# Rows of ones and zeros, a moved split and a new filler in a two-layer graph kernel

## The chip, the cores and the metric

The kernel runs on one core of a Trainium2 chip. The metric is the device time of one execution in microseconds (us), as a median of runs. The core's engines are named as in its profile: PE (matrix multiplication; PEld is its loading of weights), DVE (vector), ACT (scalar), POOL (which issues the gathers) and SP (which issues most other transfers).

## The reference

A graph of 12500 nodes with 256 features and 200000 edges passes through two layers that average over incoming edges, a last linear layer, a residual and a normalization of each row:

```python
def _sage_conv(x, src, dst, W_l, b_l, W_r):
    msgs = x[src]
    agg = jax.ops.segment_sum(msgs, dst, num_segments=N_NODES)
    deg = jax.ops.segment_sum(jnp.ones((src.shape[0],), x.dtype), dst, num_segments=N_NODES)
    mean = agg / jnp.maximum(deg, 1.0)[:, None]
    return mean @ W_l + b_l + x @ W_r

h = jax.nn.relu(_sage_conv(x, src, dst, W1_l, b1, W1_r))
h = jax.nn.relu(_sage_conv(h, src, dst, W2_l, b2, W2_r))
return _layernorm(x + (h @ W3 + b3))
```

All is float32. The edges come sorted by `dst`, which is drawn as 12500 times the square of a uniform number, so nodes with low numbers have many incoming edges; `src` is uniform.

## The kernel before

Nodes lie in 98 blocks of 128, edges in tiles of 128. There are two ways to sum the messages.

**Dense, for the nodes with many edges** (the first 1280 in layer 1, the first 1792 in layer 2), in groups of 256 nodes. `count` makes a matrix of counts, how often each source node occurs for each target node of the group, tile by tile (748 tiles over the groups): DVE makes 0/1 rows `pick` (L661: 128 partitions by w rows of 98, w being 5, 7 or 9; it says which target and which block of sources an edge has), `low` (L665: which of the 128 sources in the block; four tiles at once) and `aft` (L671: edges whose target is the one that the next tile begins with; four tiles at once). PE multiplies them into `count_ps` (L691, L706, L710), and ACT copies that into `counts` (L712; for the first 128 tiles DVE adds it, L697). `product` multiplies the counts with the table of features (L638), which lies in DRAM as three bf16 parts that add up to the float32 value (`x3_d` for x, `h3_d` for the hidden layer); the parts are made by `exact` (ACT copies at L617 and L619, DVE subtractions at L618 and L620). Each product begins with a multiplication by zero (L631), loads `rows` for two blocks at a time (L635), and has three buffers for them. `degrees` (L728) adds the counts up.

**Gathers, for all other edges.** A round gathers four tiles of 128 messages with four indirect transfers on POOL (L243) into one of four `got` buffers. PE adds each up with a 0/1 matrix (L254, `part_ps`), ACT copies the result (`some`, L259), PE sums it to nodes (L265), and DVE adds it to a ring of eight blocks (`sums`, L277). In layer 1 a further column of ones gives the degrees (L270, and L273 on DVE to the row `degs`). The first rounds of layer 1 run during the setup.

**Blocks.** When a block's sums are complete, `first_block` (layer 1, three pieces) or `last_block` (layer 2, five) computes the layer for it: transposes on PE (L839) that ACT copies (`own_t`, L842), in layer 1 the degree row turned into a column by PE (L886) with its maximum and reciprocal on DVE (L889, L890), the multiplications (L863, L865), bias and relu (L868 to L871), the stores of h and of its three parts (L896, L899), in layer 2 the last linear layer (L921) and the normalization.

**Order.** The order of PE and POOL is written out by hand; that of DVE, ACT and SP is left to a scheduler. `layer` (L562) goes through the rounds. Each round has three turns; a turn takes one piece of a block that is due, and then filler from a list of stages, as much as a written cost allots to the round. In layer 1 stage 0 is the count of group 0 together with the splitting of x (`split_rows`, 98 blocks, L622); stages 1 to 5 are the dense product and degrees of one group beside the count of the next, and the storing of counts for layer 2. Layer 2 has seven stages, one dense product each, beside the count of the last group or the loading of stored counts. The filler's costs are constants (L737: 0.7 for a block of the dense product, 1.6 for 14 matmuls of the degrees, 0.8 for a split), joined by `mixed` (L746) and spread evenly over a layer's rounds:

```python
due = dense_cost * min(1.0, (i + 1 - i0) / (n - i0 - 8))
```

Of the kernel before, what the change touches and what calls it, by code (L numbers as in the profile page):

```python
# [1 line left out]

# [5 lines left out]
F32 = mybir.dt.float32  # L8
# [13 lines left out]
P = 128  # L22
# [25 lines left out]
def by_runs(  # L48
# [79 lines left out]
    h3_d = dram.tile([P, NB, 3, D], BF16, name="h3_d")  # L128
    count_d = dram.tile([HG1 - 1, P, NB, DN], BF16, name="count_d")
# [7 lines left out]
    low_t = consts.tile([P, HC * P], BF16, name="low_t")  # L137
# [3 lines left out]
    after_t = [consts.tile([P, n], F16, name=f"after_t{g}") for g, n in enumerate(tiles_of)]  # L141
# [4 lines left out]
    steps = consts.tile([P, WIDEST * NB], F16, name="steps")  # L146
# [69 lines left out]
    class Gathers:  # L216
# [45 lines left out]
        def summed(self, gr, some, two, done):  # L262
# [6 lines left out]
            if self.width > D:  # L269
                nc.tensor.matmul(sum_ps[0:1, NC], lhsT=some[:, D:D + 1], rhs=two,  # L270
                                 start=True, stop=True)
                deg = degs[:, bass.ds(n0, P)]
                nc.vector.tensor_add(deg, deg, sum_ps[0:1, NC])  # L273
# [5 lines left out]
    with tc.tile_pool(name="setup", bufs=1) as su, \  # L279
# [154 lines left out]
        nc.vector.tensor_copy(steps, steps_f)  # L434
# [127 lines left out]
    def layer(gathers, block, n_pieces, dense, dense_cost):  # L562
# [26 lines left out]
        filler = dense(waiting)  # L589
# [8 lines left out]
        begun = gathers.hot // P  # L598
        for i in range(i0, n + 1):
            before = gathers.step()  # L600
            due = dense_cost * min(1.0, (i + 1 - i0) / (n - i0 - 8))
            for part in range(3):
# [6 lines left out]
                fill(spent + (due - spent) / (3 - part))  # L609
# [11 lines left out]

    def split_rows(b):  # L622
        t = load_rows(x, N, b, "split_sb")
        s = work.tile([P, 3, D], BF16, name="parts")
        exact(t, s, t)
        nc.sync.dma_start(x3_d[:, b], s)

    def product(g, table3, c_sb):

        ps = dense_pool.tile([P, NC, DN], F32, name="dense_ps")  # L630
        nc.tensor.matmul(ps, lhsT=zeros_b, rhs=c_sb[:, :NC, :DN], start=True, stop=False)  # L631
        for b in range(NB):
            if b % 2 == 0:
                rows = work.tile([P, 2, 3, D], BF16, name="rows", bufs=3)
                nc.sync.dma_start(rows, table3[:, b:b + 2])  # L635
# [5 lines left out]
            yield COST_DENSE  # L641
# [4 lines left out]
    def count(g, to):  # L646
# [6 lines left out]
        fours = {}  # L653

        def pick(t):
# [5 lines left out]
            nc.vector.tensor_scalar(r[:, :w * NB], steps[:, :w * NB],  # L661
                                    key_t[g][:, t - lo_g:t - lo_g + 1], None, op0=OP.is_equal)
            if t % G == 0:
                low = work.tile([P, G, P], BF16, name="low")
                nc.vector.tensor_tensor(  # L665
                    low, low_t[:, t:t + G].unsqueeze(2).to_broadcast([P, G, P]),
                    lane_b.unsqueeze(1).to_broadcast([P, G, P]), op=OP.is_equal)
                aft = None
                if t + G >= FIRST:
                    aft = work.tile([P, G, NB], BF16, name="aft")  # L670
                    nc.vector.tensor_tensor(  # L671
                        aft, after_t[g][:, t - lo_g:t - lo_g + G].unsqueeze(2).to_broadcast([P, G, NB]),
                        steps[:, :NB].unsqueeze(1).to_broadcast([P, G, NB]), op=OP.is_equal)
                fours[t // G] = low, aft
            low, aft = fours[t // G]
            return r, low[:, t % G], None if aft is None else aft[:, t % G]

        before = None
        for t in range(lo_g, highs[g]):
# [6 lines left out]
            if t < FIRST:  # L686
# [13 lines left out]
                yield count_cost(t)  # L700
            else:
                n0 = off_act.at(t)
                for a, b in halves:
# [10 lines left out]
                    yield count_cost(t) / len(halves)  # L714
# [7 lines left out]
    def degrees(g, c_sb):  # L722
# [3 lines left out]
        for j in range(DN // P):  # L726
            for b in range(NB):
                nc.tensor.matmul(ps[:, 0, j:j + 1], lhsT=c_sb[:, b, j * P:(j + 1) * P], rhs=ones_b,  # L728
                                 start=b == 0, stop=b == NB - 1)
                if b % 14 == 13:  # L730
                    yield COST_DEGREES
# [5 lines left out]
    COST_DENSE, COST_DEGREES, COST_SPLIT = 0.7, 1.6, 0.8  # L737
# [8 lines left out]
    def mixed(*parts):  # L746

        costs = [c for _, c in parts]
        scale = (max(costs) + 0.3 * (sum(costs) - max(costs))) / sum(costs)
# [568 lines left out]
```

## Time and profile before

| | |
|---|---|
| median of 10 runs | 3413.87 us (3406.39 to 3431.78) |
| the profiled execution, its own time | 3425.84 us |
| its span, from the first to the last instruction | 3424.0 us |
| mean granted PE clock | 0.860 |
| busy: PE, DVE, ACT, POOL | 2600.4, 1463.4, 1238.1, 2045.3 us |
| gathers (L243), layer 1 and layer 2 | 1076 of 1023 ns, 988 of 954 ns |
| moved from and to memory | 582.80 MB read, 89.87 MB written |

In the groups of instructions a line has the source line, the engine, the operation, output and inputs with their sizes, the count, then the busy time in us with the mean of one in ns, and after the second bar the idle time of the engine just ahead of these instructions, with what ended most of it. A line of waits has the waiting instruction, what it waited for, the total in us, the number of waits and the longest. The row PEclk has the granted clock in 40 slices of the span, in tenths of full speed.

### The profile page before, as it was taken

The numbers are of one execution on the slowest core, as the hardware profiler recorded it, in microseconds if no ns is written. First come the engines' busy times: TensorE is split into PE (matmuls) and PEld (weight loads), VectorE is DVE, ScalarE is ACT, GpSimd is POOL, SyncE is SP. The second block draws the span as 40 slices with busy tenths as digits, with TensorE's granted clock in tenths as the row PEclk, the third lists the DMA queues.
The fourth block names the chain that finished last, engine by engine and source line by source line (L and its number), as shares of the span: only waits on it lengthen the run. The fifth ranks groups of instructions, "written<-read, shape, count | busy, mean of one in ns | idle before, by whom it ended". The sixth has DMA issues, their size and how long they took to land.

```text
span 3424.0 us, 54100 instructions
## 1 busy us (share of the span) xinstructions
PE 2600.4 (76%) x18630; PEld 1709.4 (50%) x18630; DVE 1463.4 (43%) x4350; ACT 1238.1 (36%) x2702; POOL 2045.3 (60%) x2074
## 2 busy tenths in 40 slices
PE   3565547878878889889975677778778788878885
PEld 1132225546545656556653444445555565656664
DVE  5667565444444445555442123333223233333333
ACT  0323555555555555565552014333111121211212
POOL 5675655666665665665663666666666666655551
PEclk8576668888979989989987988888889999999998
DMA  4454568648648658757743665666778787766762
GB/s 114 134 148 149 167 202 271 200 144 276 201 149 270 214 156 273 214 149 224 221 136 113 193 206 175 187 191 211 244 237 253 243 252 244 242 202 207 217 203 68
DMA packets 408133, 676.44 MB, mean 198 GB/s; under 512 B 59659, under 2 KB 266537, under 8 KB 407849
## 3 DMA queue, kind: packets, MB, share of 16 engines
q1 hardware_dynamic: 303415, 400.51, 37.9%
q0 software_dynamic: 99072, 270.66, 26.3%
q8 instruction: 149, 2.44, 0.3%
q10 hardware_dynamic: 5362, 1.72, 0.3%
q14 instruction: 135, 1.11, 0.1%
HBM read 582.80 MB, written 89.87 MB: 196 GB/s over the span
## 4 chain that ended last, share of the span: by engine, by line
PE 64%; issue 10%; another core or an unknown queue 8%; DVE 7%; ACT 5%; DMA 4%; ACTq 1%; SPq 0%; DVEq 0%
PE dense_ps L638 21%; PE part_ps L254 9%; PE block_ps L863 7%; PE count_ps L706 6%; PE block_ps L865 5%; PE sum_ps L265 4%; PE block_ps L839 3%; PE block_ps L921 3%; ACT counts L712 2%; PE sum_ps L270 2%; DMA rows<-x_d 1%; PE count_ps L710 1%; DMA rows<-h_d 1%; PE block_ps L886 1%
## 5 line engine op out<-in xcount | busy, mean ns | idle before, releaser
L243 POOL DMA_INDIRECT got<-in_x_dram,src_t x1076 | 1100.5, 1023 | 702.0 <-issue 261.9
L243 POOL DMA_INDIRECT got<-h_d,src_t x988 | 942.7, 954 | 616.1 <-issue 287.1
L638 PE MATMUL dense_ps<-counts,rows 128*128 128x256 bf16 x7056 | 1022.2, 285 | 71.7 <-issue 39.7
L712 ACT CAST counts<-count_ps 128x392 f32 (+2 forms) x1052 | 716.7, 682 | 522.2 <-PE count_ps L710 117.8
L638 PEld LDWEIGHTS <-rows 128*128 128x128 bf16 x7056 | 686.1, 102 | 362.0 <-issue 176.3
L706 PE MATMUL count_ps<-pick,low 128*128 128x392 bf16 (+2 forms) x1052 | 364.4, 370 | 142.0 <-ACT counts L712 63.7
L254 PE MATMUL part_ps<-got,one 128*32 128x257 f32 (+1 forms) x4128 | 399.6, 446 | 93.1 <-ACT some L259 30.4
L661 DVE TENSOR_SCALAR pick<-steps,key_t 128x686 bf16<-128x686 f16 (+2 forms) x748 | 298.6, 410 | 215.1 <-PE count_ps L706 55.9
L201 DVE TENSOR_TENSOR one<-lo_t,lane_b 128x128 f32<-128x128 bf16 x516 | 147.9, 287 | 564.8 <-PE part_ps L254 106.2
L259 ACT COPY some<-part_ps 128x257 f32<-128x257 f32 (+1 forms) x361 | 136.1, 377 | 647.0 <-remote 169.1
L277 DVE TENSOR_TENSOR sums<-sums,sum_ps 128x256 f32 x361 | 148.3, 411 | 297.3 <-remote 118.1
L265 PE MATMUL sum_ps<-two,some 128*128 128x128 f32 x1444 | 245.9, 295 | 4.9 <-issue 4.7
L265 PEld LDWEIGHTS sum_ps<-two,some 128*128 128x128 f32 x1444 | 211.7, 207 | 35.5 <-issue 20.3
L254 PEld LDWEIGHTS part_ps<-got,one 128*32 128x32 f32 x4128 | 92.5, 115 | 254.3 <-issue 170.8
L706 PEld LDWEIGHTS <-low 128*128 128x128 bf16 x1052 | 105.3, 103 | 186.4 <-issue 87.5
L842 ACT COPY own_t<-block_ps 128x256 f32<-128x256 f32 (+1 forms) x294 | 109.8, 377 | 216.8 <-PE block_ps L839 64.6
L868 DVE TENSOR_TENSOR own<-block_ps,biases 128x256 f32<-128x256 f32 x196 | 82.6, 422 | 206.6 <-PE block_ps L865 86.8
L863 PE MATMUL block_ps<-w2l_sb,sums 128*128 128x256 f32 x336 | 115.7, 477 | 46.0 <-DVE sums L277 37.4
L863 PE MATMUL block_ps<-w1l_sb,sums 128*128 128x256 f32 x352 | 125.2, 485 | 30.7 <-DVE sums L277 15.0
L921 PE MATMUL block_ps<-w_sb,own_t 128*128 128x256 f32 x392 | 117.1, 425 | 41.4 <-ACT own_t L842 24.8
L665 DVE TENSOR_TENSOR low<-low_t,lane_b 128x512 bf16<-128x512 bf16 x187 | 128.0, 685 | 42.8 <-PE count_ps L710 13.7
L871 ACT ACTIVATE h<-own 128x256 f32<-128x256 f32 x196 | 81.4, 415 | 174.9 <-DVE own L869 94.9
(180 smaller groups left out, 2614.5 us busy)
## 6 DMA issues: line engine op xcount, KB each, us to landing
rows<-h_d SPq DMA_DIRECT2D x343, 384.0 KB
rows<-x_d SPq DMA_DIRECT2D x245, 384.0 KB
count_d<-counts SPq DMA_DIRECT2D x28, 896.0 KB
counts<-count_d SPq DMA_DIRECT2D x28, 896.0 KB
x_sb<-in_x_dram SPq DMA_DIRECT2D x194, 128.0 KB
x_d<-parts SPq DMA_DIRECT2D x98, 192.0 KB
h_d<-parts SPq DMA_DIRECT2D x98, 192.0 KB
got<-in_x_dram,src_t POOLq DMA_INDIRECT x1076
```

The costliest lines, as they stand in the source:

```text
L201: nc.vector.tensor_tensor(one, lo[:, a:a + n * (G - 1) + 1:n].unsqueeze(2).to_broadcast([P, G, W]), lane_b[:, :W].unsqueeze(1).to_broadcas ...
L243: nc.gpsimd.indirect_dma_start(out=g[:, j, :D], out_offset=None, in_=self.table, in_offset=bass.IndirectOffsetOnAxis(ap=src_t[:, e:e + 1], ...
L254: nc.tensor.matmul(part_ps[j * W:(j + 1) * W, :width], lhsT=one[:, j], rhs=g[:, j, :width], start=r == 0, stop=r == n - 1)
L265: nc.tensor.matmul(sum_ps[:, c], lhsT=some[:, c * P:(c + 1) * P], rhs=two, start=True, stop=True)
L277: nc.vector.tensor_add(own, own, sum_ps[:, :NC])
L638: nc.tensor.matmul(ps[:, c], lhsT=rows[:, b % 2, k, c * P:(c + 1) * P], rhs=c_sb[:, b, :DN], start=False, stop=b == NB - 1 and k == 2 and ...
L661: nc.vector.tensor_scalar(r[:, :w * NB], steps[:, :w * NB], key_t[g][:, t - lo_g:t - lo_g + 1], None, op0=OP.is_equal)
L706: nc.tensor.matmul(ps[:, :(b - a) * NB], lhsT=s, rhs=r[:, a * NB:b * NB], start=True, stop=alone)
L712: nc.scalar.copy(to[:, :, bass.ds(n0 + a, b - a)], ps[:, :(b - a) * NB].rearrange("p (d s) -> p s d", s=NB))
L863: nc.tensor.matmul(ps[:, 0], lhsT=agg[:, c], rhs=wl[:, c], start=c == 0, stop=c == NC - 1)
L865: nc.tensor.matmul(ps[:, 1], lhsT=own_t[:, c], rhs=wr[:, c], start=c == 0, stop=c == NC - 1)
L921: nc.tensor.matmul(y[:, 0], lhsT=h2_t[:, c], rhs=w3_sb[:, c], start=c == 0, stop=c == NC - 1)
```

## The change

Four things are changed, in this order in the diff.

First, the degree sums in layer 1 read the upper halves of their float32 operands as bf16, so that the fp32 matmul becomes a bf16 one. The degree row of a block no longer becomes a column by a matmul with one: it is stored to DRAM (`deg_d`) and loaded as a column two turns later, and the maximum and the reciprocal follow another two turns later.

Second, `pick`, `low` and `aft` are each made for one tile by an operation with one source tensor and a scalar per partition. The sources lie in rows with a gap of two elements after each (`steps` in rows of 98, `lanes_5` in five rows of 26, `steps_7` in seven rows of 14); the output is one run. The scalars of low and aft become float32.

Third, x is split during the first dense product: `product` takes its rows from a function that gives them for two blocks, ahead by one pair; for the first group the function makes the split, hands the tile to PE and stores it to `x3_d`.

Fourth, the filler's share for each round comes from a model of the load of PE, DVE and ACT for each stage and each round (`paced`), and the parts of a stage advance in equal shares (`in_turn`). Further, the `own` tile has two buffers, which `z` shares, and `h_sb` shares the tag of `split_sb`.

```diff
-    low_t = consts.tile([P, HC * P], BF16, name="low_t")
+    low_t = consts.tile([P, HC * P], F32, name="low_t")
-    steps = consts.tile([P, WIDEST * NB], F16, name="steps")
+    steps = consts.tile([P, WIDEST, NB + 2], F16, name="steps")
+    LW = 130
+    lanes_5 = consts.tile([P, 5, LW // 5 + 2], F16, name="lanes_5")
+    steps_7 = consts.tile([P, 7, NB // 7 + 2], F16, name="steps_7")
...
             if self.width > D:
-                nc.tensor.matmul(sum_ps[0:1, NC], lhsT=some[:, D:D + 1], rhs=two,
+                nc.tensor.matmul(sum_ps[0:1, NC], lhsT=some[:, D:D + 1].bitcast(BF16)[:, 1:2],
+                                 rhs=two.bitcast(BF16).rearrange("p (n h) -> p n h", h=2)[:, :, 1],
                                  start=True, stop=True)
...
-        filler = dense(waiting)
+        filler = staged(stages, waiting)
...
+        upto = [left_after(g) if r == groups[g][1] - 1 else 0 for g, r in gathers.rounds]
+        upto = [max(begun, *upto[:i + 1], 0) for i in range(n)]
+        base = [[a + x / groups[g][1] + (upto[i] - upto[max(i - 12, 0)]) / 12 * y
+                 for a, x, y in zip((0.68, 0.29, 0.0), (0.7, 0.95, 0.38), of_block)]
+                for i, (g, r) in enumerate(gathers.rounds)]
+        due = paced(stages, base[i0:n - 8])
         for i in range(i0, n + 1):
             before = gathers.step()
-            due = dense_cost * min(1.0, (i + 1 - i0) / (n - i0 - 8))
+            upto = due[min(i - i0, len(due) - 1)]
...
+    def loaded_rows(table3, b):
+        rows = work.tile([P, 2, 3, D], BF16, name="rows", bufs=3)
+        nc.sync.dma_start(rows, table3[:, b:b + 2])
+        return rows
+
     def split_rows(b):
-        t = load_rows(x, N, b, "split_sb")
-        s = work.tile([P, 3, D], BF16, name="parts")
-        exact(t, s, t)
-        nc.sync.dma_start(x3_d[:, b], s)
-
-    def product(g, table3, c_sb):
+        rows = work.tile([P, 2, 3, D], BF16, name="rows", bufs=3)
+        for k in range(2):
+            t = load_rows(x, N, b + k, "split_sb")
+            exact(t, rows[:, k], t)
+        nc.sync.dma_start(x3_d[:, b:b + 2], rows)
+        return rows
+
+    def product(g, rows_of, c_sb, whole):
...
+        following = rows_of(0)
         for b in range(NB):
             if b % 2 == 0:
-                rows = work.tile([P, 2, 3, D], BF16, name="rows", bufs=3)
-                nc.sync.dma_start(rows, table3[:, b:b + 2])
+                rows, following = following, rows_of(b + 2) if b + 2 < NB else None
...
-            nc.vector.tensor_scalar(r[:, :w * NB], steps[:, :w * NB],
+            nc.vector.tensor_scalar(r[:, :w * NB].rearrange("p (d s) -> p d s", s=NB), steps[:, :w, :NB],
                                     key_t[g][:, t - lo_g:t - lo_g + 1], None, op0=OP.is_equal)
-            if t % G == 0:
-                low = work.tile([P, G, P], BF16, name="low")
-                nc.vector.tensor_tensor(
-                    low, low_t[:, t:t + G].unsqueeze(2).to_broadcast([P, G, P]),
-                    lane_b.unsqueeze(1).to_broadcast([P, G, P]), op=OP.is_equal)
...
+            low = work.tile([P, LW], BF16, name="low", bufs=6)
+            nc.vector.tensor_scalar(low.rearrange("p (a b) -> p a b", a=5), lanes_5[:, :, :LW // 5],
+                                    low_t[:, t:t + 1], None, op0=OP.is_equal)
+            aft = None
+            if t + 1 >= FIRST:
+                aft = work.tile([P, NB], BF16, name="aft", bufs=6)
+                nc.vector.tensor_scalar(aft.rearrange("p (a b) -> p a b", a=7), steps_7[:, :, :NB // 7],
+                                        after_t[g][:, t - lo_g:t - lo_g + 1], None, op0=OP.is_equal)
+            return r, low[:, :P], aft
...
-    COST_DENSE, COST_DEGREES, COST_SPLIT = 0.7, 1.6, 0.8
+    COST_DENSE, COST_DEGREES = 0.7, 0.4
...
+    OF_DENSE = (NB * 0.7, 0.0, 0.6)
+    OF_DEGREES = (5.5, 0.0, 0.0)
+    OF_SPLITS = (0.0, NB * 0.82, NB * 0.75)
+    MOST_LOAD = (0.95, 0.88, 0.9)
...
+    def paced(stages, rounds):
+        loads = [[sum(x) for x in zip(*l)] for _, l in stages([])]
+        def by_rounds(length):
+            at, s = [], 0.0
+            for base in rounds:
+                left = 1.0
+                while s < len(loads) and left > 1e-9:
+                    of = loads[int(s)]
+                    speed = min((length * m - b) / f for m, b, f in zip(MOST_LOAD, base, of) if f)
+                    if speed <= 0:
+                        break
+                    step = min(speed * left, int(s) + 1 - s)
+                    left -= step / speed
+                    s = int(s) + 1 if step == int(s) + 1 - s else s + step
+                at.append(s)
+            return at
...
     def first_block(b, agg=None):
         x_sb = load_rows(x, N, b, "x_sb")
         of_ring = agg is None
-        yield True
-        ps = turned()
         if of_ring:
             overlap(b, True)
             agg, deg_row = ring(b)
-            nc.tensor.matmul(ps[:, NC, 0:1], lhsT=deg_row, rhs=ones[0:1, 0:1], start=True, stop=True)
-        x_t, deg = transposed(x_sb, ps, "own_t", int(of_ring))
+            nc.sync.dma_start(deg_d[b:b + 1], deg_row)
+        yield True
+        if of_ring:
+            deg = work.tile([P, 1], F32, name="deg")
+            with nc.allow_non_contiguous_dma(reason="a row becomes a column"):
+                nc.sync.dma_start(deg, deg_d[b, :, None])
+        x_t = transposed(x_sb, turned(), "own_t")
+        yield True
         if of_ring:
             nc.vector.tensor_scalar(deg, deg, 1.0, None, op0=OP.max)
             nc.vector.reciprocal(rdeg[:, b:b + 1], deg)
-        yield True
         h, own = sage(x_t, b, agg, w1l_sb, w1r_sb, biases[:, 0], "h")
...
-    layer(gathers_1, first_block, 3, staged(stages_1), cost_of(stages_1))
-    layer(Gathers(h_d, True), last_block, 5, staged(stages_2), cost_of(stages_2))
+    layer(gathers_1, first_block, 3, stages_1, (2.35, 2.0, 2.0))
+    layer(Gathers(h_d, True), last_block, 5, stages_2, (3.6, 2.6, 1.75))
```

## The prediction

> **What bounds the kernel now.** I read the page first: the shares, the slices and the chain that ended last. Then the stretches between the zero matmuls that open each dense product (L631), for busy time by stage; then the groups by shape, for prices; then the waits and the timeline around single steps.
>
> ```profile
> span 3424.0 us, 54100 instructions
> PE 2600.4 (76%) x18630; PEld 1709.4 (50%) x18630; DVE 1463.4 (43%) x4350; ACT 1238.1 (36%) x2702; POOL 2045.3 (60%) x2074
> PEclk8576668888979989989987988888889999999998
> PE 64%; issue 10%; another core or an unknown queue 8%; DVE 7%; ACT 5%; DMA 4%; ACTq 1%; SPq 0%; DVEq 0%
> ```
>
> PE carries 64% of the chain, but is not full: it is busy 76% of the span, and the clock row is low where it is least busy.
>
> ```profile
> core 0: us, PE busy (x) PEld busy (x) DVE busy (x) ACT busy (x) POOL busy (x), PEclk, DMA share, GB/s
> 90.00:300.00 210.00, 131.11 (x592) 54.63 (x596) 141.43 (x414) 59.29 (x106) 142.24 (x131) 0.65 0.49 146
> 300.00:491.00 191.00, 109.28 (x583) 51.72 (x576) 129.75 (x354) 116.80 (x244) 112.37 (x107) 0.70 0.53 161
> 491.00:716.00 225.00, 167.11 (x1228) 108.95 (x1228) 111.81 (x328) 114.29 (x230) 127.67 (x125) 0.86 0.77 236
> 716.00:778.00 62.00, 43.59 (x403) 26.20 (x403) 26.51 (x80) 32.98 (x70) 39.46 (x40) 0.72 0.38 113
> 1278.00:1475.00 197.00, 179.62 (x1366) 123.42 (x1366) 100.18 (x297) 111.16 (x238) 119.00 (x121) 0.97 0.79 243
> 1475.00:1539.00 64.00, 50.13 (x442) 30.89 (x442) 31.71 (x99) 37.50 (x77) 40.86 (x42) 0.81 0.42 121
> ```
>
> The first two rows are stage 0 of layer 1 (splits of x and counts of group 0), the next two stage 1 (dense part, then degrees), the last two stage 4. Four gathers on POOL make a round, so the rows give the time of a round: a dense stretch 197/(121/4) = 6.5 us, a degree stretch 64/(42/4) = 6.1. By PE's program order stage 0 holds 57 rounds (401 us, 7.0 each), stage 1 40 (287, 7.2), stages 2 to 5 163 (1075 with a tail of 53 us without gathers: 6.27 each), layer 2 247 (1571, tail 85). So rounds have nearly one length however much filler they hold, and stages 0 and 1 have the longest ones: there PE is waiting (busy .60 in stage 0, where DVE has .68).
>
> ```profile
> POOL got L243 <- PE part_ps L254: 252.3, 87, 19.0
> SPq L626 <- DVE parts L620: 233.0, 35, 92.5
> DVE own_t L889 <- ACT own_t L842: 44.8, 37, 9.9
> ```
>
> POOL waits for PE to free the `got` buffers (252 us in 87 waits): PE sets the pace, not the gathers. Two gathers start 1.25 us apart where nothing holds them (0.95 busy, 0.30 issue): 5 us a round.
>
> **The counts' rows.**
>
> ```profile
> L661 DVE TENSOR_SCALAR pick<-steps,key_t 128x490 bf16<-128x490 f16 x252 | 85.3, 359 | 37.3 <-PE count_ps L710 9.2 <-PE count_ps L706 8.6 <-issue 7.2
> L661 DVE TENSOR_SCALAR pick<-steps,key_t 128x882 bf16<-128x882 f16 x212 | 98.6, 467 | 73.8 <-PE count_ps L706 23.7 <-PE part_ps L254 14.2 <-PE block_ps L839 8.9
> L665 DVE TENSOR_TENSOR low<-low_t,lane_b 128x512 bf16<-128x512 bf16 x187 | 128.0, 685 | 42.8 <-PE count_ps L710 13.7 <-PE count_ps L706 8.1 <-PE part_ps L254 7.6
> L671 DVE TENSOR_TENSOR aft<-after_t,steps 128x392 bf16<-128x392 f16 x156 | 87.1, 558 | 0.0
> L270 PE MATMUL sum_ps<-two,some 128*1 128x128 f32 x372 | 77.0, 292 | 0.0
> L886 PE MATMUL block_ps<-ones,degs 1*128 1x1 f32 x176 | 39.3, 290 | 93.3 <-DVE own L869 49.9 <-issue 11.5 <-DVE degs L273 11.4
> L362 DVE CAST dst_f<-dst_i 128x1664 f32<-128x1664 int32 x1 | 1.0, 1019 | 0.0
> ```
>
> A pick costs 0.28 ns an element now ((467-359)/392). The source gets rows with gaps, an odd number of them, against one run in the output. No row shows this form. Bounds: as now (no cost), or the 1.06 ns of low and aft ((685-558)/120). Between lie the casts: 1664 elements 1019 ns, 1280 elements 827 ns, so 0.50 ns an element and 187 fixed. I take the casts, as the nearest one-source operation that isn't at the quickest rate: picks of 490, 686 and 882 then cost 432, 530 and 628 ns, 392 us for 252 + 284 + 212, against 299: +94. Low becomes 748 operations on 130 elements (252 ns by the casts: 188 us against 128, +60), aft 621 on 98 (236 ns: 147 against 87, +60). DVE +214 in all. By the lower bound (two 128x128 tensor-scalars of the setup took 201 ns) it is about +60, by the upper (1.06 ns and 187 fixed for all) 675-299, 243-128 and 181-87, about +586.
>
> [...]
>
> Off the path: DVE is busy .50 in stage 4; with the 120-tile share of +214 (34 us) it is .63. In stage 0 it is 271 of 401 us; the splits leave (98 x 0.85 = 83), nine rounds leave (about 11), 236 tiles' share comes (+68): 245 us, in 307 (below) .80, still covered. [...] Gathers took 1023 ns in layer 1 and 954 in layer 2; were the picks the cause, 0.07 x 1076 = 75 us of POOL's time come back, which isn't late; I take none.
>
> **The degrees.** L270's 372 fp32 passes become 186 bf16 matmuls: 77 us of PE to 186 x 0.22 = 41 (0.22 us is the mean of the nearest bf16 matmul, aft's 128x98 of L710), 36 saved, between nothing, if light rounds keep their length anyway, and 77. Of the 186 groups 133 lie in stages 2 to 5 (83 groups of two rounds come first, then 103 of one): 26 us there. L886 leaves PE with its 93 us of waits on DVE: 33 of them in stage 0, 32 in stage 1, 20 in stages 2 to 5 where gathers run. In place of it each of 88 blocks issues on SP a 512-byte store behind DVE's add and a 4-byte-packet load. What is queued behind that store on SP: rows loads, h_d and h3_d stores, x_sb loads; PE's dense product waits for rows, but three buffers hold two pairs ahead. A small load takes 2.5 us from issue to use (the split's, shown below: 546.23 to 548.72), the pair about 5; the block asks for the result four turns later (four thirds of a round, 8.4 us). I take 0. Upper bound: SP's longest hold at a rows load is 10.9 us; 10.9 + 5 - 8.4 = 7.5, for a block in four 165 us. Lower bound: 0, as PE's side is counted already.
>
> **The splits move.** Stage 0 loses 98 splits with their 98 loads and 98 stores; SP's 233 us of waits on their last subtraction shrink with them, and PE's one wait of 10 us behind ACT's part of a split in stage 0. Stage 1 gets them, per pair of blocks: two loads, eight operations on ACT and DVE, one store in place of two, and no reading back (49 loads of 384 KB fall away; PE waited 9 us for them). The timeline of stage 1 shows one block's chain from load issue to last subtraction:
>
> ```profile
> 546.23 0.45 SPq L833 DMA_DIRECT2D split_sb<-in_x_dram  x1
> 548.72 0.40 ACT L617 CAST parts<-split_sb 128x256 bf16<-128x256 f32 x1 [0.74 <-DMA split_sb<-in_x_dram]
> 550.27 0.43 DVE L620 TENSOR_TENSOR parts<-split_sb,parts 128x256 bf16<-128x256 f32 x1 [0.35 <-ACT parts L619]
> ```
>
> That is 550.70 - 546.23 = 4.5 us. With two buffers the second block's chain overlaps the first's by half: 4.5 + 2.3 = 6.8 a pair. One pair is emitted ahead. Price: 49 x 6.8 = 331 us for stage 1.
>
> **The filler.** A new pacing moves the stages: by PE's program order after, stage 0 has 48 rounds, stage 1 48, stages 2 to 5 164, layer 2 247. Degree stretches, which were allotted 10 rounds for 196 matmuls of 25 ns, get fewer.
>
> **The sum** on the span: setup 90. Stage 0: (401 - 33 - 10)/57 = 6.3, with DVE's higher share 6.4, x 48 = 307 (-94). Stage 1: (287-32)/40 = 6.4 a round is the floor, 6.9 with the chain, x 48 = 331 (+44). Stages 2 to 5: the light rounds' 6.1 less L270's saving (26/163) = 5.95, x 164 + 53 = 1029 (-46). Layer 2: 1571 less 30, as its last stages (198 us, 31.5 rounds, 6.3) come down toward the 6.1 of its long second one = 1541 (-30). Together -126. The profiled execution took 3425.84 (span 3424.0): 3300; it lies 12 above the median of 3413.87, so 3288.
>
> **Rivals.** A: evening out lets the gathers set the pace. POOL's 2043 us of gathers and 2064 gaps of 0.30 are 2662 us, 5.16 a round; halfway from 6.2 is 5.7, x 507 + 90 + 53 + 85 + 26 (starts of layer 2) = 3144, median 3134. For: PE's waits on L886 vanish. Against: rounds with next to no filler took 6.1. [...] C, slower: the chain of the pair in stage 1, serial through SP (a store that waits for DVE stands before the next two loads). It decides from (331+126)/49 = 9.3 us a pair, where it takes back all that the sum gains; two chains one after the other take 9.0, and with two issues on SP held for a microsecond each 11: 539 us, +208, 3496. For it: SPq waited up to 92.5 us on that subtraction. Against: two buffers and one pair's lead. D: nothing measurable: the round stays what it is, since it hardly depends on filler, and stage 1 takes back what stage 0 gives: 3414.
>
> **The numbers.** Forecast .56, A .15, B .11, C .12, D .06. Faster (by over 0.3%, about what a measurement of this kernel can tell): forecast, A and B, .82; within, D, .06; slower, C, .12. From 3130 (A's middle) to 3405 (B whole, and the degree loads' bound in most part) leaves out half of A and C, 0.2.
>
> **What would show it.** Right: picks near 432/530/628 ns, stage 0 near 307 us and stage 1 near 331, no PE wait on degrees, rounds of stages 2 to 5 near 5.95. Wrong: picks of 490 at 359 or at 706; the zero matmul of group 1's product near 940 instead of 728 (C); DVE waiting for the degree column; POOL with no waits on part_ps (A).

## The result, and the profile after

The changed kernel takes 3609.89 us (median of 9 runs, 3594.01 to 3616.06), the kernel before 3415.01 in the runs beside it: a ratio of 1.0555 (95% interval 1.0535 to 1.0575). It is slower, by 195 us, where 3288 was forecast, outside the range of 3130 to 3405. The ratios below are all against runs of the kernel before on the same chip; that matters, since not all chips ran it alike (see the end).

The page of the profile after, the same rows as before:

```profile
span 3598.1 us, 54700 instructions
PE 2609.0 (73%) x18268; PEld 1695.0 (47%) x18268; DVE 1625.8 (45%) x5378; ACT 1249.7 (35%) x2702; POOL 1983.7 (55%) x2074
PEclk9677777768989988989987898888888889889888
PE 58%; issue 11%; another core or an unknown queue 9%; DVE 9%; DMA 7%; ACT 5%; SPq 1%; DVEq 0%; ACTq 0%; POOL 0%; POOLq 0%
```

PE is busy as long as before (2609 against 2600 us, with the 362 matmuls of the degrees fewer) in a span that is 174 us longer: what was added is idle time of PE. In the chain DMA went from 4 to 7% and DVE from 7 to 9%. The stretches between the zero matmuls (now L658) show where:

```profile
core 0: us, PE busy (x) PEld busy (x) DVE busy (x) ACT busy (x) POOL busy (x), PEclk, DMA share, GB/s
90.00:419.00 329.00, 203.25 (x1012) 83.55 (x1013) 257.60 (x871) 124.64 (x198) 199.30 (x206) 0.74 0.33 97
419.00:840.00 421.00, 269.94 (x1689) 140.51 (x1688) 222.31 (x753) 200.93 (x446) 186.00 (x191) 0.72 0.54 166
1338.00:1626.00 288.00, 233.10 (x1777) 160.62 (x1777) 156.01 (x531) 154.61 (x322) 161.61 (x170) 0.86 0.66 198
2364.00:2557.00 193.00, 140.76 (x1024) 97.26 (x1023) 43.00 (x131) 22.57 (x63) 104.55 (x110) 0.87 0.75 228
```

These are stage 0 after the setup, stage 1, stage 4, and layer 2's third stage. By stage, in us of the span (each column one profiled run; the last three are from experiments told below, the changed kernel once more, with its transfers unweighted, and with the loads of x early as well, on a chip that runs the kernel before in 3411 us):

| | before | forecast | after | after, repeated | transfers unweighted | and loads early |
|---|---|---|---|---|---|---|
| setup and stage 0 | 491 | 397 | 419 | 421 | 424 | 411 |
| stage 1 | 287 | 331 | 421 | 426 | 374 | 303 |
| stages 2 to 5 | 1075 | 1029 | 1130 | 1128 | 1078 | 1090 |
| layer 2 | 1571 | 1541 | 1628 | 1638 | 1570 | 1576 |
| span | 3424 | 3298 | 3598 | 3612 | 3446 | 3380 |

The first gain came nearly as forecast; stage 1 paid three times what was forecast (134 us against 44), and everything behind it, layer 2 included, became slower instead of faster. In layer 2 neither the rows of ones and zeros (but for one stage) nor the degrees nor the split is at work. The filler is, and so are the shared buffers and the loads of rows that are emitted a pair ahead; the run with the old filler, below, tells them apart.

The groups by shape and the waits, after (the last line is of before):

```profile
L687 DVE TENSOR_SCALAR pick<-steps,key_t 128x490 bf16<-128x490 f16 x252 | 113.9, 459 | 60.2 <-remote 15.0 <-PE count_ps L727 13.6 <-PE count_ps L731 10.5
L687 DVE TENSOR_SCALAR pick<-steps,key_t 128x882 bf16<-128x882 f16 x212 | 141.1, 666 | 72.3 <-PE part_ps L262 21.2 <-remote 17.6 <-PE count_ps L727 12.3
L690 DVE TENSOR_SCALAR low<-lanes,low_t 128x130 bf16<-128x130 f16 x748 | 201.5, 271 | 128.8 <-remote 36.2 <-PE count_ps L731 24.1 <-PE part_ps L262 20.2
L695 DVE TENSOR_SCALAR aft<-steps,after_t 128x98 bf16<-128x98 f16 x621 | 156.8, 253 | 0.1
L279 PE MATMUL sum_ps<-two,some 128*1 128x128 bf16 x186 | 42.3, 228 | 0.4 <-issue 0.3
```

```profile
POOL got L251 <- PE part_ps L262: 498.1, 145, 14.0
PE dense_ps L665 <- DMA rows<-h_d: 85.3, 45, 7.1
PE dense_ps L665 <- ACT rows L636: 63.8, 25, 10.9
```

```profile
PE dense_ps L638 <- DMA rows<-h_d: 21.8, 16, 3.4
```

The prices of the single operations were right: picks 459 and 666 ns (432 and 628 forecast), low 271 (252), aft 253 (236), the bf16 degree matmul 228 (220). POOL's wait for PE doubled (252 to 498 us), and PE has two long waits, one larger than before and one new: for rows of h (85 us, 21.8 before) and, in stage 1, for ACT's first copy of a split.

### The profile page after: what moved, and what is told of

Read it like the earlier page. It is cut to its first block, busy times and chain, and to the rows that moved or that the text cites. A ratio compares the mean times of both kernels' runs of the same rounds, so it can differ in the third digit from the quotient of the medians.

```text
span 3598.1 us, 54700 instructions
## 1 busy us (share of the span) xinstructions
PE 2609.0 (73%) x18268; PEld 1695.0 (47%) x18268; DVE 1625.8 (45%) x5378; ACT 1249.7 (35%) x2702; POOL 1983.7 (55%) x2074
## 4 chain that ended last, share of the span: by engine, by line
PE 58%; issue 11%; another core or an unknown queue 9%; DVE 9%; DMA 7%; ACT 5%; SPq 1%; DVEq 0%; ACTq 0%; POOL 0%; POOLq 0%
PE dense_ps L665 19%; PE part_ps L262 8%; PE block_ps L916 7%; PE count_ps L727 6%; PE block_ps L918 5%; PE sum_ps L273 4%; DMA rows<-h_d 3%; PE block_ps L977 3%; PE block_ps L893 2%; ACT counts L733 2%; DVE pick L687 2%; PE count_ps L731 1%; DMA split_sb<-in_x_dram 1%; DVE low L690 1%
## 5 line engine op out<-in xcount | busy, mean ns | idle before, releaser
L251 POOL DMA_INDIRECT got<-in_x_dram,src_t x1076 | 1043.8, 970 | 881.7 <-PE part_ps L262 312.2
L665 PE MATMUL dense_ps<-counts,rows 128*128 128x256 bf16 x7056 | 1068.3, 295 | 252.8 <-DMA rows<-h_d 85.3
L727 PE MATMUL count_ps<-pick,low 128*128 128x392 bf16 (+2 forms) x1052 | 377.2, 383 | 195.6 <-ACT counts L733 100.0
L687 DVE TENSOR_SCALAR pick<-steps,key_t 128x686 bf16<-128x686 f16 (+2 forms) x748 | 414.3, 556 | 229.9 <-remote 68.5
L690 DVE TENSOR_SCALAR low<-lanes,low_t 128x130 bf16<-128x130 f16 x748 | 201.5, 271 | 128.8 <-remote 36.2
L273 PEld LDWEIGHTS sum_ps<-two,some 128*128 128x128 f32 x1444 | 219.7, 212 | 51.0 <-issue 33.3
L895 ACT COPY own_t<-block_ps 128x256 f32<-128x256 f32 x294 | 109.8, 375 | 295.0 <-PE block_ps L893 79.8
L695 DVE TENSOR_SCALAR aft<-steps,after_t 128x98 bf16<-128x98 f16 x621 | 156.8, 253 | 0.1
L893 PE MATMUL block_ps<-ident,h 128*128 128x128 f32 x196 | 46.8, 325 | 136.8 <-ACT h L924 95.6
```

The costliest lines, as they stand in the source:

```text
L251: nc.gpsimd.indirect_dma_start(out=g[:, j, :D], out_offset=None, in_=self.table, in_offset=bass.IndirectOffsetOnAxis(ap=src_t[:, e:e + 1], ...
L273: nc.tensor.matmul(sum_ps[:, c], lhsT=some[:, c * P:(c + 1) * P], rhs=two, start=True, stop=True)
L665: nc.tensor.matmul(ps[:, c], lhsT=rows[:, b % 2, k, c * P:(c + 1) * P], rhs=c_sb[:, b, :DN], start=False, stop=b == NB - 1 and k == 2 and ...
L687: nc.vector.tensor_scalar(r[:, :w * NB].rearrange("p (d s) -> p d s", s=NB), steps[:, :w, :NB], key_t[g][:, t - lo_g:t - lo_g + 1], None, ...
L690: nc.vector.tensor_scalar(low.rearrange("p (a b) -> p a b", a=5), lanes_5[:, :, :LW // 5], low_t[:, t:t + 1], None, op0=OP.is_equal)
L695: nc.vector.tensor_scalar(aft.rearrange("p (a b) -> p a b", a=7), steps_7[:, :, :NB // 7], after_t[g][:, t - lo_g:t - lo_g + 1], None, op0 ...
```

## The experiments

**First, each part undone in the changed kernel.** The four ran beside the kernel before on one chip.

The rows of ones and zeros as before:

```diff
-            low = work.tile([P, LW], BF16, name="low", bufs=6)
-            nc.vector.tensor_scalar(low.rearrange("p (a b) -> p a b", a=5), lanes_5[:, :, :LW // 5], ...
+            if t % G == 0:
+                low = work.tile([P, G, P], BF16, name="low")
+                nc.vector.tensor_tensor(low, ...   # as before; pick and aft likewise
```

> The changed kernel with pick, low and aft made as before (one source run, low and aft for four tiles at once); the rest of the change stays. Theory DVE: the +259 us of busy DVE (picks at 459/561/666 ns) hold the counts, so the time falls by about 90 us to 3520, 20 in stage 0 (DVE .91 busy there) and 70 in stages 2 to 5, whose rounds go from 6.93 back toward 6.5; layer 2 gains only in the one stage that counts. Theory filler: rounds are long because of where they were moved; no more than 20 us fall, to 3590.

Measured: 3576.86 us, 1.0473 (1.0449 to 1.0496): 33 us, not 90, and no stage stands out (stage 0 417 against 419, stage 1 414 against 421, stages 2 to 5 1125 against 1130). The rows are not the main cause. (The .91 of the expectation is not in the row of stage 0 above: DVE is busy 257.6 of 329 us there, .78.)

The degree column on PE again:

```diff
-            nc.sync.dma_start(deg_d[b:b + 1], deg_row)
...
-                nc.sync.dma_start(deg, deg_d[b, :, None])
+            nc.tensor.matmul(ps[:, NC, 0:1], lhsT=deg_row, rhs=ones[0:1, 0:1], start=True, stop=True)
```

> The changed kernel with the degree row turned into a column by PE again, beside the transposes (the bf16 degree sums stay). Theory SP: the 88 stores that wait on DVE's add hold SP (86 us of waits) and so the rows; without them 30 to 60 us are won: 3560. Rival, in which the column by transfer is a gain as predicted: PE's waits on the row return, some 50 to 90 us: 3680.

Measured: 3593.04 us, 1.0542 (1.0503 to 1.0581), which can't be told from the changed kernel's 1.0555. Both expectations missed: the column by transfer neither costs nor gains.

The splits back in stage 0:

```diff
+            if g == 0:
+                parts.append(splits())
+                loads.append(OF_SPLITS)
...
-                parts.append(dense(g - 1, split_rows if g == 1 else partial(loaded_rows, x3_d),
+                parts.append(dense(g - 1, partial(loaded_rows, x3_d),
```

> The changed kernel with the splits of x back in stage 0 as a part of their own (with their load in the model of the filler), and all products reading x in three parts from memory. Theory chain: stage 1 is paced by the split of a pair (8.6 us a pair, 421 us); without it stage 1 falls below 300, stage 0 grows by about 80 us for its DVE work: net -60, 3550. Rival: DVE in stage 0 is full already (.91), so stage 0 grows by as much as stage 1 loses: 3610.

Measured: 3533.41 us, 1.0359 (1.0326 to 1.0391). Stage 1 falls from 421 to 253 us (with 33 rounds instead of 47.5) and stage 0 grows from 419 to 542 (82 rounds instead of 61.5). The move costs some 70 us net, near the theory's 60; of the profiled run's 74, 44 lie in these two stages and 26 in stages 2 to 5.

The old filler:

```diff
-        due = paced(stages, base[i0:n - 8])
+            due = dense_cost * min(1.0, (i + 1 - i0) / (n - i0 - 8))   # and mixed, the costs, as before
```

> The changed kernel with the old filler: constant costs, one share for all rounds. Theory filler: layer 2 falls from 1628 back to about 1571, and stages 2 to 5 by some 40 us, to 3510. Rival, in which layer 2 lost by the earlier emission of rows or by the buffers: layer 2 stays at 1628, and the time within 20 us of 3610.

Measured: 3487.23 us, 1.0217 (1.0193 to 1.0242): the largest of the four. Layer 2 comes back to 1562 us, with the shared buffers and the rows emitted ahead still in place, so that the filler alone is the cause there. In stage 1 the dense product falls from 399 us to 326, while the degree sums behind it take 62 us, about as before the change, instead of 22. So two parts cost most, the filler first, then the moved split.

**Then each part alone in the kernel before.**

The degrees (bf16 sums, and the column by transfer):

> The kernel before with the bf16 degree sums and the column by transfer. As I predicted it, PE's waits on the row (93 us) and 36 us of matmuls go: 3340. Rival from the run without the column, in which the transfers cost 17 us: SP is held behind DVE and the gain is lost, 3400 to 3430.

Measured: 3409.40 us, 0.9984 (0.9959 to 1.0008): no difference. The trace shows where the waits went. PE's groups of the transposes, first before, then with this part alone:

```profile
L839 PE MATMUL block_ps<-ident,x_sb 128*128 128x128 f32 x196 | 49.9, 343 | 0.9 <-ACT own_t L842 0.7 <-DVE own L869 0.2
```

```profile
L851 PE MATMUL block_ps<-ident,x_sb 128*128 128x128 f32 x196 | 45.5, 317 | 58.3 <-DVE own L880 53.0 <-DVE pick L676 2.4 <-issue 1.6
```

The transposes had 0.9 us of idle time ahead of them and now have 58.3, 53 of it for DVE's `own`. That is the wait that stood at L886 (49.9 us for `own`). It was never for the degree row: `own` is computed from the block before in `block_ps`, which has two buffers, and whichever instruction is first to write the buffer waits for that. Removing the first instruction handed the wait to the next.

In the changed kernel the wait isn't at the transposes either:

```profile
L893 PE MATMUL block_ps<-ident,x_sb 128*128 128x128 f32 x196 | 44.2, 312 | 3.8 <-DVE own L922 2.0 <-DMA x_sb<-in_x_dram 1.3 <-ACT own_t L895 0.5
```

There `own` has two buffers, and the splits have left stage 0. Each by itself takes most of the wait away: with the moved split alone PE waits 0.2 us for `own` in such a place, with the two buffers and the splits in stage 0 (the run of the rows alone) 13.1 us.

The moved split, alone:

```diff
-                rows = work.tile([P, 2, 3, D], BF16, name="rows", bufs=3)
-                nc.sync.dma_start(rows, table3[:, b:b + 2])
+                rows, following = following, rows_of(b + 2) if b + 2 < NB else None
...
-                parts.append((splits(), NB * COST_SPLIT))
```

> The kernel before with the splits in the first product (rows emitted a pair ahead), old filler with its 40 rounds for stage 1. Theory chain: the pair's split takes 6 to 8 us in series (store behind DVE, then the loads), stage 1 grows from 287 to 390 and stage 0 loses 70: 3440. Rival: with DVE's rows as before the chain is short, stage 1 near 310, 3370.

Measured: 3465.73 us, 1.0175 (1.0120 to 1.0229): stage 0 426 us (-65), stage 1 385 (+98). The two stages are as the theory of the chain has them; the total lies 26 us above its 3440. Of the 385 us the dense product takes 322, and the degree sums behind it 63. One link of the chain in the changed kernel's timeline (start, duration, engine; the lines between them are of other work):

```profile
600.75 0.32 SPq L652 DMA_DIRECT2D x_d<-rows  x1
601.12 0.93 SPq L888 DMA_DIRECT2D split_sb<-in_x_dram  x2
...
605.21 0.71 ACT L636 CAST rows<-split_sb 128x256 bf16<-128x256 f32 x2
605.64 0.76 DVE L637 TENSOR_TENSOR split_sb<-split_sb,rows 128x256 f32<-128x256 f32 x2
605.66 0.39 PE L665 MATMUL dense_ps<-counts,rows 128*128 128x256 bf16 x2 [1.11 <-ACT rows L636]
606.10 0.74 ACT L638 CAST rows<-split_sb 128x256 bf16<-128x256 f32 x2 [0.18 <-DVE split_sb L637]
606.53 0.76 DVE L639 TENSOR_TENSOR rows<-split_sb,rows 128x256 bf16<-128x256 f32 x2
...
606.99 0.33 SPq L652 DMA_DIRECT2D x_d<-rows  x1
```

From one store of a pair to the next 6.2 us, of which 3.2 pass between the end of the issue of the loads (602.05) and ACT's first copy (605.21). SP issues the loads of the next pair only after the store of this one, and the store waits for DVE's last subtraction (97.6 us in 23 waits over the stage). Counted in the trace from store to store, the links of the changed kernel take 7.3 us in the median; but five of the 47 take 16 us and more, so that the mean is 8.4. The dense product takes 399 of the stage's 421 us. With the move alone the mean link is 6.9 us, and in the changed kernel with the old filler 6.9 as well, none longer than 13.5.

The new filler, alone:

> The kernel before with only the new filler. Its splits would be modelled in stage 0, as in the run with the splits back. Theory filler: layer 2 grows by 57 to 66 us (1571 to 1630), layer 1 by 0 to 50: 3480 to 3530. Rival, in which it is only bad together with the moved split: 3415.

Measured: 3546.33 us, 1.0385 (1.0353 to 1.0417). It costs 132 us without any other part; layer 2 takes 1641 us, layer 1 1919 against 1853.

The rows of ones and zeros, alone (with the shared buffers of the change: without them the work tiles need 30.375 KB of a partition, where 27.875 are left), on another chip:

> The kernel before with only the new pick, low and aft, and the shared buffers of the change (own, z, h_sb), which it needs to fit. Theory DVE is a side cost: +20 to +40 us, most of it in stages 0 and 1, where DVE is fullest: 3445. Rival: no cost, or a gain from POOL's shorter gathers (970 instead of 1023 ns in layer 1, 57 us), 3400 to 3415.

Measured: 3368.10 us, 0.9946 (0.9925 to 0.9968) beside 3386.58 on that chip. No loss, the rival's side: DVE has room for the 257 us more that the rows keep it busy, and layer 1's gathers take 973 ns instead of 1023. Whether the small gain is the rows' is not shown, since `own` has its second buffer here too. With 33 us lost in the changed kernel and none here, the sign depends on what else runs.

**What in the filler costs.** Layer 2 was run without its loads of rows, with the old filler and with the new one. Both kernels multiply the first pair's rows again and again.

```diff
     def loaded_rows(table3, b):
+        if table3 is h3_d and b > 0:
+            return kept[-1]
```

> The kernel before, of whose layer 2 the loads of rows are left out but for the first of each product (the product then multiplies the same rows again; its result is not the reference's). A control for the next run: if transfers bound the dense stages of layer 2 (242 to 249 GB/s there), layer 2 falls from 1571 to 1500 or less; if rounds are bound by PE and its waits, it stays within 20 us.

Measured: 3376.67 us, 0.9977 (0.9957 to 0.9996); layer 2 1556 us, where the run above, with its loads and on the same chip, has 1554. With the old filler the loads cost next to nothing.

> The kernel before with the new filler (as in the run of the filler alone, layer 2 1641 us), and the same loads of rows of layer 2 left out. Theory transfers: the new filler took rounds out of stages that their rows and counts bound (190 us each, however many rounds), so without these loads its stages shrink with their rounds and layer 2 comes to the control's time or below. Rival: the rounds themselves cost more where they were moved (heavy stages by PE's waits, light rounds no less than 6.2 us), and layer 2 stays 50 to 70 us above the control.

Measured: 3452.71 us, 1.0198 (1.0153 to 1.0243); layer 2 1564 us, 8 above the control, where the filler alone had stood 70 above. (What is left of the loss lies in layer 1, whose loads were kept: 1888 us against 1819.) So the loss in layer 2 comes through the loads of rows, as the theory of the transfers has it. But its reason, rounds moved out of those stages, didn't fit everything: in the changed kernel the stages of layer 2 without a loading of counts were about as quick per round as before (144 us for 23.5 rounds, 250 for 40, about 6.2 each), and only those with it were slow. Layer 2's third stage takes 193 us for 27.5 rounds, 7.0 each; the kernel before takes 191 for 31, 6.2 each:

```profile
2365.00:2556.00 191.00, 148.97 (x1084) 105.47 (x1084) 51.29 (x155) 26.23 (x74) 117.25 (x124) 0.88 0.77 238
```

So I counted the dense blocks of each round in PE's program order, in layer 2's fourth stage, first before and then after:

```
3 3 3 4 2 4 3 3 3 3 3 4 3 2 4 3 3 3 3 3 4 3 2 4 3 3 3 3 3 4 3 3
0 4 7 3 0 3 7 3 0 4 6 4 0 2 7 5 0 1 8 5 0 0 6 8 0 0 6 6 3
```

Here it lies. `in_turn` gives every part of a stage an equal share of the filler. The loading of counts is a part, of seven transfers that cost PE nothing, and each uses up 1/14 of the stage's filler, about two rounds, in which PE gets no dense block; then 6 to 8 come in one round and run into the loads of their rows, of which three buffers hold two pairs ahead. The third stage has the same pattern. In layer 1 the storing of counts does the same with 1/21.

The correction lets transfers count nothing:

```diff
-                yield share / len(parts)
+                yield 0.0 if p[2] else share / work_parts   # p[2]: the part is stored or loaded
```

> The kernel before with the new filler, in which the storing and loading of counts no longer uses up a share of the filler (they are issued in turn, and count nothing). In the changed filler each of seven transfers of a stage counts as 1/21 (layer 1) or 1/14 (layer 2) of the stage, so that by PE's program order 9 to 14 rounds of a layer 2 stage hold no block of the dense product and others hold 6 to 8. Theory bursts: this is all of the filler's loss (+132 us alone), and goes: layer 2 from 1641 to 1575 or less, the time within 20 us of the kernel before or below it. Rival: the load model itself is wrong, since it takes rounds out of stages that the loads of rows bound; then layer 2 stays above 1600 and the time 70 us above the kernel before.

Measured: 2850.39 us beside 2908.31 of the kernel before: 0.9811 (0.9770 to 0.9851). This and the next three ran on a chip that runs the kernel before in 2908 us instead of 3414, and so prove nothing by their times against the runs above. The uncorrected filler was not run there; the ladder below has both on one chip.

> The changed kernel with the same single correction of the filler. Theory bursts: 110 to 130 us fall, to +2 or +2.5% over the kernel before; what is left is stage 1. Rival: the other parts bring waits of their own, less than 60 us fall.

Measured: 2896.77 us, 0.9958 (0.9930 to 0.9987), below what was expected; but it was expected of a chip of the other kind.

For the chain of the split, the loads were put ahead of the store:

```diff
-        for k in range(2):
-            t = load_rows(x, N, b + k, "split_sb")
+        for c in (b, b + 2):
+            if c < NB and c not in at_hand:
+                at_hand[c] = [load_rows(x, N, c + k, "split_sb") for k in range(2)]
+        for k, t in enumerate(at_hand.pop(b)):
             exact(t, rows[:, k], t)
         nc.sync.dma_start(x3_d[:, b:b + 2], rows)
```

> The kernel before with the splits in the first product, as in the run of the move alone (3466, stage 1 385 us), and with x's loads issued a pair earlier, ahead of the store that waits for DVE (four load buffers, for which own, z and h_sb share theirs). Theory chain through SP: the 3 us of load latency per pair leave the chain, stage 1 comes from 385 to about 310, the time to 3390. Rival: ACT and DVE work set the chain, stage 1 stays above 370, 3460.

Measured: 3329.94 us, 0.9824 (0.9796 to 0.9852) beside 3386.58; stage 0 427 us, stage 1 271. On this chip the kernel before takes 486 and 281 in these stages (read from the run that differs from it in layer 2 alone). PE's waits in stage 1 with the move alone, then with the early loads:

```profile
PE dense_ps L649 <- ACT rows L620: 68.2, 37, 3.4
PE dense_ps L649 <- ACT rows L622: 22.6, 39, 1.9
```

```profile
PE dense_ps L653 <- ACT rows L622: 7.5, 5, 2.6
```

Of 91 us of waits for ACT's two copies 7.5 are left, and the mean link from store to store goes from 6.9 us to 4.4. The order on SP was the cause; ACT and DVE work was not. (The four buffers belong to the order: without them the loads can't go ahead. The second buffer of `own` came with them, and its share is not shown.)

Both corrections in the changed kernel, and the parts that gained put together with the old filler, on the quick chip:

> The changed kernel with the corrected filler, and with the loads of x for the split issued a pair ahead of the store (four load buffers; one buffer for h's parts and five for low to make room). If the two causes found are all, stage 1 falls by another 100 us, and the time comes 0.5 to 1.5% below the kernel before. If rows and column cost more together than alone, it stays above.

Measured: 2792.28 us, 0.9625 (0.9576 to 0.9674), below what was expected.

> The kernel before with the parts that gained alone: new pick, low and aft (-0.5%), splits in the first product with early loads (-1.8%), and bf16 degree sums (not run alone; with the column -0.2%); old filler, column on PE. If the gains add up: 2.3 to 2.8% below the kernel before, 3325 where that is 3414.

Measured: 2829.72 us, 0.9728 (0.9682 to 0.9774), as expected; on that chip the corrected filler and the column by transfer, which only the run above has, are together worth another 1%.

**The ladder.** The changed kernel, the first correction and both, on one chip (the kernel before 3410.88):

> The changed kernel itself, for a ladder on one chip with the next two (the last four runs were on a chip where the kernel before takes 2908 us instead of 3414). Where the kernel before takes about 3400: 1.05 to 1.06 of it. Where it takes about 2900 and GpSimd's gathers set the pace in light rounds: theory bursts still costs, 1.02 to 1.05; if the loss is a matter of a slow PE only, about 1.00.

Measured: 3610.07 us, 1.0565 (1.0523 to 1.0607).

> The changed kernel with the corrected filler again, beside the changed kernel. Theory bursts: at least 2.5% below the run beside it (110 to 130 us of 3610), with the loss all in stages that store or load counts. If the 0.996 measured before came from the chip, it is within 1% of it.

Measured: 3444.23 us, 1.0089 (1.0061 to 1.0117): 166 us less, 162 of them in the eight stages that store or load counts. Layer 2's third stage, first uncorrected, then corrected, with the same 1024 matmuls:

```profile
2370.00:2574.00 204.00, 148.40 (x1024) 100.88 (x1023) 42.69 (x131) 23.10 (x64) 104.96 (x111) 0.87 0.69 216
```

```profile
2269.00:2437.00 168.00, 135.56 (x1024) 94.90 (x1023) 42.91 (x131) 22.10 (x63) 104.59 (x111) 0.94 0.83 262
```

36 us of 204 go. 13 of them are PE's own busy time, at a granted clock of .94 instead of .87; the rest is idle time. In stage 1 the mean link of the split falls from 8.5 us to 7.3, and the longest from 17.8 to 11.4: the long links were the bursts' as well. PE's wait for rows of h goes from 87.5 us to 36.6 over the run:

```profile
PE dense_ps L665 <- DMA rows<-h_d: 87.5, 49, 6.3
```

```profile
PE dense_ps L665 <- DMA rows<-h_d: 36.6, 30, 2.9
```

No run here shows why the granted clock is .87 with the bursts and .94 without.

> The changed kernel with the corrected filler and the early loads again, beside the two. Theory chain: stage 1 another 100 us shorter than beside it, 3% of the kernel before; with both causes gone the time is 1.5 to 4% below the kernel before, on a chip of either kind.

Measured: 3381.94 us, 0.9912 (0.9883 to 0.9942): another 62 us, 71 of them in stage 1 (374 to 303 us). With both causes gone the changed kernel is faster than the one before, by 0.9% here and 3.8% on the quick chip. Of 199 us lost 166 were the bursts, and 62 the loads behind the store; what the change gains without these two, 29 us, was hidden under them.

## Why the prediction was wrong

**The filler** is the step that failed. The prediction counted rightly how many rounds each stage has in PE's program order (48, 48, 164, 247), but it has no term for how the work lies inside a stage: it took it to be spread evenly over the rounds, as it is before. On this it gave -30 us in layer 2, and about -20 of the -46 in stages 2 to 5 (26 are the degree sums'). Measured were +57 and +55. The same program order, looked at by round instead of by stage, would have shown the zeros and eights, and the diff has the cause in one line: an equal share for each part, where a cost weighted it before. With the transfers unweighted, stages 2 to 5 and layer 2 are at 1078 and 1570 us: the forecast's gains are not there either, only the loss is gone. So the second half of that step, that evening out brings heavy rounds down to the light ones, was wrong as well on this kind of chip; rounds stay at 6.05 to 6.25 us in layer 2's corrected stages (168/27.8, 200/32.2), about what they were.

In all, 314 us lie between the forecast's span, 3298, and that of the repeated run, 3612. The bursts are 166 of them. The other 148 are there with the transfers unweighted too: 27 in the setup and stage 0, 43 in stage 1, 49 in stages 2 to 5, 29 in layer 2.

**The split in stage 1** was priced at 6.8 us a pair, 331 us for 49 pairs; the stage took 421. The price of the chain was right in sum: the mean link is 6.9 us with the old filler, alone and in the changed kernel. Its parts were not, which is luck: in the timeline of the experiments 3.2 us pass from the loads' issue to the first copy (2.0 in the prediction's), and the second block adds less than half a chain. Two things were missing from the stage. The degree sums behind the product belong to the stage, too, and 49 pairs cover the product alone: 22 us. And the bursts reach the chain: the product takes 399 us, 402 in the repeated run and 345 with the transfers unweighted. Rival C named the mechanism, a store that waits for DVE ahead of the next loads on SP, but priced it at 11 us, with 0.12; the forecast's own sum had the chain as well, at a better price. That the early loads win 71 us in the stage shows that the chain does bound it.

**The degrees.** Of the 93 us of waits at L886 the sum booked 65 as removed, in stages 0 and 1. The line itself said that 49.9 of the 93 were for `own`, a DVE result that has no part in the degrees, and it was the buffer's: alone the part only moved them to the transposes. Only the waits on `degs` (11 us in that line) belonged to the row. In the changed kernel the transposes have 3.8 us of idle time, so the waits are gone, and the time is no shorter for it: with the column on PE again it is the same within the spread. The matmul's price was right (42.3 us for 186, 41 forecast), and the 35 us of PE saved showed nowhere: 3409 against 3414 us alone.

**Right:** the rows' prices (+259 us of DVE against +214) and, but for 33 us in the changed kernel, that DVE covers them (alone, with the shared buffers, they cost nothing); stage 0, 419 us against 397, with 6.9 us a round instead of 6.4; the column's transfers at 0. Rival A's state, the gathers setting the pace, exists: on the quick chip layer 2's second stage takes 203/39.8 = 5.1 us a round in the kernel before with the corrected filler; POOL waits 1.5 us for `part_ps` there, and PE 27 us for gathers. Rival B (.11), DVE at the upper bound's 1.06 ns an element (+586 us), no run shows: picks cost 0.53 ns an element, and the pick of 490 took 459 ns, not 706.

With the rows with gaps an element of a pick went from 0.28 to 0.53 ns ((666-459)/392), nearly double and close to the 0.50 of the casts; no run shows why. That low and aft became 1369 operations in place of 343 cost little here: alone there was no loss, and undoing all the new rows in the changed kernel won 33 us.

## What to carry to other kernels

When filler is spread by a model, print how much work each step of the program gets, not only how much each stage gets; a part that costs nothing must count nothing. A wait listed at an instruction belongs to what it names as the releaser: if that has nothing to do with the instruction's own data, ask whether it is a buffer's. Here it was, and it moved to the next instruction (49.9 us at L886, then 53.0 at the transposes). On SP a store that waited for a result stood before the loads for the next one; turned round, a stage of 374 us took 303.

## What was not expected of the hardware

One of the four chips ran the kernel before in 2908 us where three others took 3387 to 3415, at a granted PE clock of .92 instead of .87. The same program, corrected filler in the changed kernel, has a span of 2893 us there and 3446 elsewhere. PE is 2360 us busy instead of 2573, which is 213 of the 553 us between them; the rest is idle time that isn't there. The other engines are busy as long on both (DVE 1622 us on each, POOL 1984 and 1981). On the slower chips 8 to 12% of the chain are put down to "another core or an unknown queue", on the quick one none; the same program, with the early loads, first there, then elsewhere:

```profile
PE 41%; DMA 26%; POOL 10%; DVE 10%; issue 8%; ACT 4%; ACTq 0%; DVEq 0%; SPq 0%; POOLq 0%
```

```profile
PE 60%; issue 11%; DVE 9%; another core or an unknown queue 9%; DMA 5%; ACT 4%; POOL 1%; DVEq 0%; ACTq 0%; SPq 0%; POOLq 0%
```

What those pauses are the records don't say, and no run was made for it: it stays open, and with it why the corrected changed kernel gains 3.8% there and 0.9% here.
